# A three-layer GCN with an attention layer: layers as adj @ (h @ W), operands supplied transposed, bias and ReLU in one activation

## Chip, cores, metric

One core of a Trainium2 chip. The metric is the device time of one execution in microseconds (us), the median of several runs. Spans and durations come from the profile of one execution; a span is some 1.8 us shorter than the time of the same execution.

## The reference, cut

64 graphs of 256 nodes, 512 features, all float32.

```python
# layer 0: three GCN layers, then residual and layer norm
h = relu(adj @ (x @ W1) + b1)
h = relu(adj @ (h @ W2) + b2)
x = layernorm(x + adj @ (h @ W3) + b3)
# layer 1: graph attention with one weight per node
q, k = split(x @ Wqk);  v = x @ Wv
agg = adj @ (k * mask)
w = mask / sqrt(512) * rowsum(q * agg)
x = layernorm(x + softmax_over_nodes(w) * v)
```

Both kernels form M = Wq Wk^T once on the chip, so that w = mask/sqrt(512) * rowsum((x M) * (adj @ (mask x))).

## The kernel before

TensorE multiplies a stationary `lhsT` (transposed) by a moving `rhs`. The columns counted below are those of `rhs`. Two graphs (a pair) are handled together, and layer 1 of a pair ends inside the next pair's turn.

```python
    def transpose_adj(i, aj, k):
        pt = psum.tile([P, NH, N], FP, name="pa", tag="mm")
        for m in range(NH):
            for h in range(NH):
                nc.tensor.transpose(pt[:, m, h * P:(h + 1) * P], aj[:, k, h, m * P:(m + 1) * P], ident)
        aT = work.tile([P, NH, N], FP, name="aT", bufs=4)
        nc.scalar.copy(aT, pt)
        # ... aTm = aT times the mask, on GpSimd

    def aggregate(h_in, aT):                  # (adj @ h).T, features on partitions
        # ... for f, m:
                    nc.tensor.matmul(pz[:, j, :], lhsT=h_in[:, m, f * P:(f + 1) * P], rhs=aT[:, m, :], ...)
        # ... pz copied to zT, half by VectorE and half by ScalarE

    def project(srcT, w, h):                  # 128 rows of src @ w
        for f in range(DC):
            nc.tensor.matmul(pp, lhsT=srcT[:, f, h * P:(h + 1) * P], rhs=w[:, f, :], ...)

    def hidden(zT, n):
        # ... pp = project(zT, wl[n], h)
            nc.vector.tensor_tensor(t, pp, bl[n], op=OP.add)
            nc.scalar.activation(hn[:, h, :], t, AF.Relu)

    for i in range(NP + 1):
        # ... loads of pair i + 1
            aTs = [transpose_adj(i, aj, k) for k in ks]
        if last is not None:
            sm = softmax_rows(last[2])        # transposes the scores (pw), softmax
        if i < NP:
            zs = [aggregate(xt[:, k], aTs[k][0]) for k in ks]
        # ...
        if last is not None:
            s = softmax_cols(sm)              # transposes back (ps)
            for k in ks:
                layer1_out(i - 1, k, last[0][k], last[1][k], s)   # x1 @ Wv, sum, norm, store
        # ... two hidden layers, layer 3, layer norm, scores of pair i
```

## Time and profile before

| | before |
|---|---|
| time, us (first three runs; 3231.38 with the fourth) | 3231.34 (3231.33 to 3231.42) |
| span of the profiled run, us | 3230.6 |
| TensorE busy | 100% |
| VectorE, ScalarE, GpSimd busy | 32%, 17%, 9% |
| one pair of graphs in the steady state, us | 99.85 |

The page's first part gives busy time by engine (PE is TensorE, PEld its weight loads, DVE VectorE, ACT ScalarE, POOL GpSimd); the slices show whether that holds throughout; the chain says what the end of the program waited for. The prediction shows the lines. In the chain in order of time a row is start, length and what ran: with a TensorE that never rests, the chain accounts for the whole time of the program.

### The profile page before, as it was taken

How to read it: one execution, taken by the hardware profiler on the slowest of the kernel's cores; microseconds unless marked ns; L12 is line 12 of the kernel's file. 1: busy time of each engine (PE TensorE's matmuls, PEld its weight loads, DVE VectorE, ACT ScalarE, POOL GpSimd, SP SyncE). 2: the span in 40 equal slices, each digit the busy share in tenths (PEclk: the TensorE clock that was granted, in tenths of full speed). 3: DMA queues.
4: the chain of work that ended last, by engine and by line, in shares of the span. 5: the costliest groups of instructions: out<-in, count | busy, mean ns of one | idle time of the engine just before them, and what ended most of it. 6: DMA issues, size and time to landing. Idle time of an engine off the chain costs nothing.

```text
span 3230.6 us, 23926 instructions
## 1 busy us (share of the span) xinstructions
PE 3215.3 (100%) x9666; PEld 1753.3 (54%) x9666; DVE 1033.9 (32%) x2055; ACT 561.7 (17%) x970; POOL 276.0 (9%) x262
## 2 busy tenths in 40 slices
PE   8999999999999999999999999999999999999999
PEld 5555555555555555555555555555555555555554
DVE  1332323323333233233332332323323333333233
ACT  2111111111111111111111111111111111111111
POOL 1110011110111101111001110011110111101110
PEclk9999999999999999999999999999999999999999
DMA  3110001000000000010000000001000001000000
GB/s 134 33 33 20 26 20 33 33 20 26 20 33 33 20 26 21 32 33 26 26 27 20 33 30 23 26 20 33 33 20 26 20 33 33 20 26 20 26 14 13
DMA packets 54509, 92.55 MB, mean 29 GB/s; under 512 B 2240, under 2 KB 18688, under 8 KB 54400
## 3 DMA queue, kind: packets, MB, share of 16 engines
q1 hardware_dynamic: 54400, 91.04, 8.3%
q8 instruction: 76, 1.25, 0.2%
q14 instruction: 33, 0.27, 0.0%
HBM read 57.48 MB, written 33.55 MB: 28 GB/s over the span
## 4 chain that ended last, share of the span: by engine, by line
PE 100%; DMA 0%; DVE 0%; SPq 0%; DVEq 0%; issue 0%; ACT 0%
PE pp L150 68%; PE pz L138 21%; PE pg L208 7%; PE px L193 2%; PE pa L121 1%; PE pt L113 0%; PE pw L224 0%; PE ps L239 0%; DMA mask_n<-in_nodemask 0%; PE pt L103 0%; DVE r L248 0%; DVE st L167 0%; DVE o L174 0%; SPq L49 0%; DVEq L304 0%
## 5 line engine op out<-in xcount | busy, mean ns | idle before, releaser
L150 PE MATMUL pp<-w,zT 128*128 128x512 f32 x3072 | 1334.0, 592 | 0.0
L150 PEld LDWEIGHTS pp<-w,zT 128*128 128x128 f32 x3072 | 583.7, 190 | 707.4 <-issue 704.1
L138 PE MATMUL pz<-aT,hn 128*128 128x256 f32 x2048 | 452.5, 379 | 0.0
L150 PE MATMUL pp<-m_qk,x1T 128*128 128x512 f32 x1024 | 449.9, 592 | 0.0
L150 PE MATMUL pp<-wv,x1T 128*128 128x512 f32 x1024 | 448.3, 595 | 0.0
L138 PEld LDWEIGHTS pz<-aT,hn 128*128 128x128 f32 x2048 | 389.1, 190 | 80.2 <-issue 30.6
L159 DVE TENSOR_TENSOR t<-pp,b 128x512 f32<-128x512 f32 x256 | 177.1, 692 | 626.5 <-PE pp L150 626.5
L127 POOL TENSOR_SCALAR aTm<-aT,mask_t 128x256 f32<-128x256 f32 x128 | 117.0, 932 | 2817.8 <-ACT aT L123 2817.8
L150 PEld LDWEIGHTS pp<-m_qk,x1T 128*128 128x128 f32 x1024 | 194.6, 190 | 244.9 <-issue 244.9
L150 PEld LDWEIGHTS pp<-wv,x1T 128*128 128x128 f32 x1024 | 191.8, 190 | 229.5 <-issue 229.0
L160 ACT ACTIVATE hn<-t 128x512 f32<-128x512 f32 x256 | 161.3, 630 | 782.0 <-DVE t L159 782.0
L141 DVE COPY zT<-pz 128x512 f32<-128x512 f32 x192 | 132.9, 692 | 470.2 <-PE pz L138 470.2
L216 DVE SCALAR_TENSOR_TENSOR prod<-pp,mask_s,g 128x512 f32<-128x512 f32 x128 | 96.1, 751 | 499.2 <-PE pp L150 499.2
L138 PE MATMUL pz<-aT,xt 128*128 128x256 f32 x1024 | 231.3, 384 | 0.0
L208 PE MATMUL pg<-x,aTm 128*128 128x512 f32 x512 | 230.3, 592 | 0.0
L138 PEld LDWEIGHTS pz<-aT,xt 128*128 128x128 f32 x1024 | 193.2, 191 | 31.0 <-ACT aT L123 5.6
L170 ACT ACTIVATE sd<-mv,eps 128x2 f32<-128x2 f32 x128 | 37.9, 296 | 836.8 <-DVE mv L168 836.8
L167 DVE BATCH_NORM_STATS2 st<-r 128x6 f32<-128x512 f32 x256 | 177.5, 693 | 7.7
L248 DVE SCALAR_TENSOR_TENSOR r<-pp,s,x 128x512 f32<-128x512 f32 x128 | 96.1, 751 | 219.4 <-PE pp L150 219.4
L143 ACT COPY zT<-pz 128x512 f32<-128x512 f32 x192 | 111.6, 581 | 296.2 <-PE pz L138 296.2
L269 POOL TENSOR_TENSOR xt<-xt,b 128x512 f32<-128x512 f32 x128 | 159.3, 1264 | 25.1 <-PE pz L138 20.4
L181 DVE TENSOR_TENSOR r<-pp,xt 128x512 f32<-128x512 f32 x128 | 88.5, 692 | 227.5 <-PE pp L150 218.9
(45 smaller groups left out, 893.2 us busy)
## 6 DMA issues: line engine op xcount, KB each, us to landing
xt<-in_x SPq DMA_DIRECT2D x32, 1024.0 KB, 5.4
out<-o SPq DMA_DIRECT2D x64, 512.0 KB, 2.8
aj<-in_adj SPq DMA_DIRECT2D x32, 512.0 KB, 3.8
w<-in_L_gnn_W SPq DMA_DIRECT2D x3, 1024.0 KB, 10.6
wqk<-in_L_gnn_Wqk SPq DMA_DIRECT2D x4, 512.0 KB, 11.9
wv<-in_L_gnn_Wv SPq DMA_DIRECT2D x1, 1024.0 KB, 12.3
b<-in_L_gnn_b SPq DMA_DIRECT2D x3, 256.0 KB, 11.1
mask_n<-in_nodemask SPq DMA_DIRECT2D x1, 64.0 KB, 6.2
```

The source lines that it names most:

```text
L127: nc.gpsimd.tensor_scalar(aTm[:, m, :], aT[:, m, :], mask_t[:, m, b:b + 1], None, op0=OP.mult)
L138: nc.tensor.matmul(pz[:, j, :], lhsT=h_in[:, m, f * P:(f + 1) * P], rhs=aT[:, m, :], start=(m == 0), stop=(m == NH - 1))
L141: nc.vector.tensor_copy(zT[:, 2 * fp:2 * fp + 2, :], pz)
L143: nc.scalar.copy(zT[:, 2 * fp:2 * fp + 2, :], pz)
L150: nc.tensor.matmul(pp, lhsT=srcT[:, f, h * P:(h + 1) * P], rhs=w[:, f, :], start=(f == 0), stop=(f == DC - 1))
L159: nc.vector.tensor_tensor(t, pp, bl[n], op=OP.add)
L160: nc.scalar.activation(hn[:, h, :], t, AF.Relu)
L167: nc.vector.bn_stats(st[:, h, :], src[:, h, :])
L208: nc.tensor.matmul(pg, lhsT=aTm[:, m, h * P:(h + 1) * P], rhs=x1[:, m, :], start=(m == 0), stop=(m == NH - 1))
L216: nc.vector.scalar_tensor_tensor(prod, py, mask_s[:, h, b:b + 1], gs[h], op0=OP.mult, op1=OP.mult, accum_out=w[:, h, k:k + 1])
L248: nc.vector.scalar_tensor_tensor(r[:, h, :], pv, s[:, h, k:k + 1], x1[:, h, :], op0=OP.mult, op1=OP.add)
L269: nc.gpsimd.tensor_tensor(xt[:, k, h, :], xt[:, k, h, :], bl[2], op=OP.add)
```

## The change

Its intent: take the adjacency transposes off TensorE, make bias and ReLU one ScalarE instruction that reads PSUM, and use wide matmuls in layer 3. To that end the features go through W first, and x and the adjacency are laid out transposed by the host. Cut to its core:

```diff
+    def product(srcT, w, name):
+        dst = work.tile([P, NH, PAIR, D], FP, name=name, tag="prod", bufs=3)
+        # ... for g, m: pp = four matmuls over f, lhsT=srcT[:, f, g, m-th 128], rhs=w[:, f, :]
+                if m:
+                    nc.vector.tensor_copy(dst[:, m, g, :], pp)
+                else:
+                    nc.scalar.copy(dst[:, m, g, :], pp)
+    def aggregate_relu(s, aT, bc):
+        # ... for f, g, m:
+                    nc.tensor.matmul(pz[:, g, :], lhsT=s[:, m, g, f * P:(f + 1) * P], rhs=aT[:, g, m, :], ...)
+            nc.scalar.activation(hT[:, f], pz, AF.Relu, bias=bc[:, f:f + 1])
+    def aggregate_residual(s, aT, xb):
+        # ... for g, n, m:
+                    nc.tensor.matmul(pr, lhsT=aT[:, g, m, n * P:(n + 1) * P], rhs=s[:, m, g, :], ...)
+                nc.vector.tensor_tensor(xb[:, g, n, :], pr, xb[:, g, n, :], op=OP.add)
-    # transpose_adj, aggregate, project, hidden (shown above)
     for i in range(NP + 1):
+        # with x, aT, rows of x loaded for pair i; "last" is pair i - 1
+            s1 = product(xt, w1, "s1")
+            x1T = transpose_x1(x1)                    # last
+            hT = aggregate_relu(s1, aT, b1c)
+            y = product(x1T, m_qk, "y")               # last
+            scores(i - 1, x1, y, aTm, w)              # last
+            v = product(x1T, wv, "v")                 # last
+            sm = softmax(w)                           # last
+            s2 = product(hT, w2, "s2")
+            s = softmax_cols(sm)                      # last
+            layer1_out(i - 1, x1, v, s)               # last
+        hT = aggregate_relu(s2, aT, b2c)
+        s3 = product(hT, w3, "s3")
+        aggregate_residual(s3, aT, xn)
+        layernorm(x1, xn)
```

## The prediction

> **What bounds the kernel now.** I read the page's busy table and slices first, then the chain that ended last, then the groups, then that chain in order of time for one pair of graphs and for the end. The page says that TensorE never rests:
>
> ```profile
> PE 3215.3 (100%) x9666; PEld 1753.3 (54%) x9666; DVE 1033.9 (32%) x2055; ACT 561.7 (17%) x970; POOL 276.0 (9%) x262
> PE   8999999999999999999999999999999999999999
> PEclk9999999999999999999999999999999999999999
> PE 100%; DMA 0%; DVE 0%; SPq 0%; DVEq 0%; issue 0%; ACT 0%
> ```
>
> Line one is busy us, share and instructions of each engine; the fourth is the chain by engine. VectorE, ScalarE, GpSimd and the DMA are a third busy or less and absent from the chain. Only three things can move the time: fewer columns through TensorE, a new gap on it, and the two ends. The groups (busy, mean ns) of the parts concerned:
>
> ```profile
> L150 PE MATMUL pp<-w,zT 128*128 128x512 f32 x3072 | 1334.0, 592 | 0.0
> L138 PE MATMUL pz<-aT,hn 128*128 128x256 f32 x2048 | 452.5, 379 | 0.0
> L121 PE MATMUL pa<-ident,aj 128*128 128x128 f32 x256 | 34.1, 277 | 0.0
> ```
>
> The last column but one is the trap. 3072 times 592 ns is 1819 us, but the group was busy 1334 us: consecutive matmuls overlap, so the mean of one is not what it costs. The chain in order of time (start, length, what) gives the step; here from one pair of the steady state:
>
> ```profile
> 113.77 0.87 PE pa L121 x8
> 114.64 0.30 PE pw L224 x2
> 114.95 7.11 PE pz L138 x32
> 122.06 0.21 PE ps L239 x2
> 122.27 27.66 PE pp L150 x64
> 149.93 6.91 PE pz L138 x32
> 156.84 13.73 PE pp L150 x32
> 191.21 0.87 PE px L193 x8
> 192.08 3.44 PE pg L208 x8
> ```
>
> A 512-column record steps by 13.73/32 = 0.429 us, a 256-column one by 6.91/32 = 0.216 us (half), a 128-column transpose by 0.109 us. Cost is columns, nothing per instruction. (A matmul of the program leaves two records, a transpose one.) One pair lasts 222.12 - 122.27 = 99.85 us, from the same chain; 32 pairs are 3195 us of the 3231.
>
> **What the Trainium skill says.** "FP8 and Floating Point Precision", section "TensorE Precision Notes", says that true FP32 takes four passes through the array. The trace agrees: two records of 0.429 us for 512 columns are 1.68 ns per column; four passes at the 2.4 GHz that "TensorE: Matmul & The Clock Gate" gives for a busy array would be 1.67. The same page, section "What happens when you issue a matmul", says that the next weights are loaded while a matmul streams. The trace agrees down to 256 columns: a weight load lasts 190 ns, the 256-column step is 216 ns. Its section "The HAM clock gate" says that the array runs at half clock until some 3.4 us of work have passed, and again after idleness of that length. The first transposes and first aggregate agree: 1.90 us against 0.87 and 8.72 us against 6.91. The granted clock row doesn't show it. "Perfetto Trace Analysis", section "Matmuls", says that larger matmuls are more efficient; between 256 and 512 columns of this kernel the trace doesn't show that.
>
> **The change part by part**, per pair, by the chain's steps.
>
> Association. Before, each of three layers is 32 records of 256 columns (aggregate) and 32 of 512 (project). Afterwards each is the same 32 of 512 first; layers one and two then aggregate with 32 of 256, features on partitions again. Swapping the order saves no arithmetic, because the width is 512 in and out. Layer three aggregates with 16 records of 512: 16 x 0.429 = 6.86 us in place of 6.91. Saved: 0.05 us.
>
> Adjacency transposes: 8 transposes, 0.87 us, gone and on the path. Saved: 0.87 us. With them goes one ScalarE copy per graph (589 ns), off the path.
>
> Softmax. The scores' row transpose (pw) now follows the product with Wv, so it no longer waits for the last score: 0.30 us becomes about 0.21. Saved: 0.09 us. The 0.2 us that TensorE loses after each of these tiny transposes (7.11 against 6.91, 27.66 against 27.46) I leave in.
>
> Bias and ReLU. 256 VectorE additions (692 ns, 177 us) and 256 ScalarE activations (630 ns, 161 us) become 256 ScalarE activations straight from PSUM, but all five products are now copied out, half by each engine. None of it is on the path: ScalarE idles 782 us ahead of its old ReLU and VectorE 627 us ahead of its addition, waiting for others.
>
> Loads. 0.5 + 1 MB in per pair become 2.5 MB; with 1 MB out that is 3.5 MB in 99 us, some 37 GB/s, against 384 GB/s moved in the busiest stretch at the start. Hidden. Single buffers: the row copy of x is reloaded only after the layer norm of the pair before, but is needed most of a period later; a 1 MB load lands in 5.4 us.
>
> Sum in the middle: 0.87 + 0.05 + 0.09 = 1.01 us, times 32 = 32 us less.
>
> Start. Before, TensorE begins at 8.1 us, when the mask lands. Now it needs W1 and x transposed, 2.1 MB, where 1.6 MB lay ahead of the mask; 0.5 MB at 385 GB/s is 1.3 us. Then the mask must land before the first aggregate; with 6 MB ahead of it that is near 20 us, and the first product ends near 25. Cost: 1.3 us, the half-clock start being paid in both.
>
> End. Here is the chain after the last matmuls of before:
>
> ```profile
> 3213.79 9.65 PE pp L150 x22
> 3223.44 0.03 issue
> 3223.47 0.76 DVE r L248
> ...
> 3225.73 0.55 DVE o L174
> 3226.28 0.46 DVEq L304
> ```
>
> From TensorE's end to the end of the span are 7.2 us: the softmax is hidden under the product with Wv, and only one graph's half and its layer norm stick out. The change serialises this. First, there is no new pair to fill in for the layer norm of layer 0: last addition 0.69, statistics 0.69 + 0.18, square root 0.30, reciprocal 0.17, four scalings of 0.54 and hand-overs: 4.3 us of idle TensorE, then perhaps half clock for one window, 1.7 us. Second, softmax follows everything: maximum 0.41, exponential 0.47 + 0.18, reciprocal 0.15, scaling 0.39, hand-overs: 1.8 us; column transposes drained and copied 0.4; then for four half-graphs 3.0 of weighted sums, 3.5 of statistics, 0.5 root and reciprocal, 2.1 scaling: about 11.5 us in all. Third, one store of 1 MB rather than two of 0.5: 3.9 us plus 0.5 MB at 385 GB/s is 5.3. So 16.8 in place of 7.2. Cost of the end: 9.6 + 4.3 + 1.7 = 15.6 us.
>
> Total: 3231.3 - 32.3 + 1.3 + 15.6 = 3215.9 us. About half of the middle's gain is given back at the ends. I say 3215.
>
> **The rivals.**
>
> Wider matmuls pay. By the means of 592 and 379 ns, layer three would save 32 x 379 - 16 x 592 = 2.7 us per pair, 85 us in all; with the transposes that makes about 3110 us, faster by over 3%. Against it stands the overlap shown above: the steps are 0.429 and 0.216. I give it two in a hundred.
>
> A new wait on ScalarE. In the instruction order of the changed kernel, the square root of the layer-1 norm stands between the third and fourth ReLU of the second aggregate, and the third layer's product needs all four. Counting from the end of the second product: VectorE copies 0.7, takes the softmax columns 0.2, four weighted sums 3.0, statistics 3.5 and the root comes at about 7.9 us. The fourth aggregate is done at 0.2 + 6.9 = 7.1, its ReLU then ends at 8.5; TensorE needs it three matmuls (six records, 2.6 us) after 7.1, at 9.7. So 1.2 us of slack. If VectorE ran 2 us longer there, TensorE would lose some 0.8 us per pair, 25 us: 3240, still within 2%. That this must cost over 3 us per pair to be slower by 2% makes it unlikely.
>
> The small stalls go. If the 0.2 us after the row and column transposes came from the transposed adjacency or the old order, up to 0.4 us per pair would go too: 13 us, 3202.
>
> A late load. The order of the queue puts the store of one pair between loads of the next. For a load to hold TensorE up it would have to land over 60 us late; the profile shows 5.4 us for 1 MB. If it happened each pair the time would exceed 3300.
>
> **Range and chances.** Work that cannot go away is 192 records of 0.429, 64 of 0.216 and 16 transposes, with pw and ps 98.4 us per pair; with the preparation of Wq Wk^T (3.49 + 13.74 us) and no gaps but the start, that is over 3170, so faster by 2% (under 3168) is all but excluded. The range runs from all small stalls gone and a cheaper end (3198) to half a microsecond more of new stalls per pair with the end as worked out (3226). Faster 0.02, same 0.965, slower 0.015.
>
> **What would show each step.** Right: TensorE again near 100%, the period near 98.8 us; adjacency transposes absent; the new 512-column aggregates step 0.43 us and the whole third aggregate lasts 6.9 us; weights loaded behind matmuls as before; VectorE idle ahead of its copies, waiting for TensorE; a gap near 4 us ahead of the last pair's transposes of x1, and 16 to 17 us from the last product to the end. Wrong: TensorE waiting each pair for the fourth ReLU or for a load; a period under 98.2 or over 99.5 us; an end as short as before; the third aggregate clearly under 6.8 us.

## The result

3205.81 us (3205.10 to 3205.96, 4 runs) against 3231.38: ratio 0.992, 95% interval 0.9906 to 0.9934, within 2%. A ratio is the mean time of one kernel's fast runs over that of the other's of the same rounds, so not quite the ratio of the medians quoted. The time lies inside the range and 9 us under the 3215 predicted.

Busy table, slices and chain by engine of the changed kernel, as shown of before:

```profile
PE 3177.7 (99%) x8898; PEld 1629.2 (51%) x8898; DVE 903.7 (28%) x1863; ACT 523.7 (16%) x842; POOL 274.8 (9%) x262
PE   8999999999999999999999999999999999999997
PE 99%; DVE 0%; DMA 0%; issue 0%; ACT 0%; DVEq 0%; SPq 0%
```

TensorE still sets the time; only its last slice has fallen, from 9 to 7. Its chain through a pair in the steady state:

```profile
246.18 0.22 PE pw L165 x2
246.40 13.74 PE pp L89 x32
260.13 0.21 PE ps L180 x2
260.34 7.10 PE pz L104 x32
...
281.18 6.87 PE pr L115 x16
...
303.53 6.91 PE pz L104 x32
```

The adjacency transposes (pa) are gone. The row transpose of the scores takes 0.22 us instead of 0.30, and what follows it loses nothing (13.74); what follows the column transpose (ps) still loses 0.2 us (7.10 against 6.91). The wide aggregate of layer 3 (pr) takes 6.87 us for 16 records, the narrow ones 6.91 for 32. From 161.75 to 3119.48 us lie 30 pairs: 98.59 us each, against 99.85, measured likewise from 122.27 to 3117.66. That is 1.26 us less, 37.7 us in 30 pairs. The span fell by 26.5 only, so the two ends gave 11 us back. The end of the changed kernel in the same chain: the gap ahead of the last pair's transposes of x1, the first product after it and the last one:

```profile
3149.51 0.56 DVE x L132
3150.07 0.04 issue
3150.11 3.05 PE px L141 x16
3153.19 14.52 PE pp L89 x32
...
3174.58 13.75 PE pp L89 x32
```

TensorE stood 2.9 us for the layer norm (the waits say PE px waited for DVE x once, 2.9 us), then the transposes took 3.05 us instead of 1.75 and the product 14.52 instead of 13.73: 5.0 us in all. The slow stretch is a lower granted clock: here are three stretches of the changed kernel, 3150.10 to 3150.86 us, 3150.86 to 3154.27 and 3154.27 to 3157.00, as the profile sums them up: length, busy time of each engine in the order of the page, and, third from the right, the granted clock.

```profile
3150.10:3150.86 0.76, 0.75 (x7) 0.71 (x8) 0.76 (x2) 0.00 (x0) 0.00 (x0) 1.00 0.03 11
3150.86:3154.27 3.41, 3.38 (x14) 2.46 (x13) 1.85 (x4) 1.07 (x2) 0.00 (x0) 0.50 0.00 0
3154.27:3157.00 2.73, 2.73 (x8) 1.30 (x7) 0.00 (x0) 0.00 (x0) 0.00 (x0) 1.00 0.00 0
```

From the end of the last product, 3188.3 us, to the end of the span are 15.8 us, against 7.2 before: 8.6 more.

### The profile page after: what moved, and what is told of

It is laid out like the page before. It is cut to its first block, busy times and chain, and to the rows that moved or that the text cites. A ratio compares the mean times of both kernels' runs of the same rounds, so it can differ in the third digit from the quotient of the medians.

```text
span 3204.1 us, 21715 instructions
## 1 busy us (share of the span) xinstructions
PE 3177.7 (99%) x8898; PEld 1629.2 (51%) x8898; DVE 903.7 (28%) x1863; ACT 523.7 (16%) x842; POOL 274.8 (9%) x262
## 4 chain that ended last, share of the span: by engine, by line
PE 99%; DVE 0%; DMA 0%; issue 0%; ACT 0%; DVEq 0%; SPq 0%
PE pp L89 69%; PE pz L104 14%; PE pg L155 7%; PE pr L115 7%; PE px L141 2%; PE pt L223 0%; DMA xt<-in_xT 0%; PE ps L180 0%; PE pw L165 0%; DVE st L124 0%; PE pt L213 0%; DVE xn L117 0%; DVE x L188 0%; DVE x L132 0%; DVE mv L125 0%
## 5 line engine op out<-in xcount | busy, mean ns | idle before, releaser
L89 PE MATMUL pp<-w,hT 128*128 128x512 f32 x2048 | 889.4, 592 | 0.0
L89 PEld LDWEIGHTS pp<-w,hT 128*128 128x128 f32 x2048 | 386.7, 190 | 462.1 <-issue 459.7
L104 PE MATMUL pz<-aT,s 128*128 128x256 f32 x2048 | 455.9, 381 | 0.0
L89 PE MATMUL pp<-w,xt 128*128 128x512 f32 x1024 | 447.7, 595 | 8.1 <-DMA xt<-in_xT 8.1
L92 DVE COPY s<-pp 128x512 f32<-128x512 f32 x192 | 132.8, 692 | 1006.4 <-PE pp L89 1006.4
L104 PEld LDWEIGHTS pz<-aT,s 128*128 128x128 f32 x2048 | 384.1, 190 | 50.6 <-issue 0.5
L89 PEld LDWEIGHTS pp<-w,xt 128*128 128x128 f32 x1024 | 195.6, 191 | 254.4 <-issue 254.4
L267 POOL TENSOR_TENSOR xn<-xn,b3r 128x512 f32<-128x512 f32 x128 | 158.0, 1265 | 1920.0 <-DMA xn<-in_xN 1902.5
L94 ACT COPY s<-pp 128x512 f32<-128x512 f32 x192 | 112.5, 586 | 798.9 <-PE pp L89 798.9
L115 PE MATMUL pr<-s,aT 128*128 128x512 f32 x512 | 224.9, 592 | 0.0
```

What stands on the lines that cost most here:

```text
L89: nc.tensor.matmul(pp, lhsT=srcT[:, f, g, m * P:(m + 1) * P], rhs=w[:, f, :], start=(f == 0), stop=(f == DC - 1))
L92: nc.vector.tensor_copy(dst[:, m, g, :], pp)
L94: nc.scalar.copy(dst[:, m, g, :], pp)
L104: nc.tensor.matmul(pz[:, g, :], lhsT=s[:, m, g, f * P:(f + 1) * P], rhs=aT[:, g, m, :], start=(m == 0), stop=(m == NH - 1))
L115: nc.tensor.matmul(pr, lhsT=aT[:, g, m, n * P:(n + 1) * P], rhs=s[:, m, g, :], start=(m == 0), stop=(m == NH - 1))
L267: nc.gpsimd.tensor_tensor(xn[:, g, h, :], xn[:, g, h, :], b3r, op=OP.add)
```

## The experiments

Theory: TensorE pays for every column in turn. The transposes are the gain, the rest of the change is neutral in the middle, and its end costs 13 us. Rivals: the gain comes from association, wide matmuls or the fused activation; the transposes were hidden; the end is set by the store.

### The transposes alone

The kernel before, with the adjacency laid out by the host.

```diff
-                nc.tensor.transpose(pt[:, m, h * P:(h + 1) * P], aj[:, k, h, m * P:(m + 1) * P], ident)
-        aT = work.tile([P, NH, N], FP, name="aT", bufs=4)
-        nc.scalar.copy(aT, pt)
+        aT = aj[:, k]
```

> The kernel before with one part of the change alone: the adjacency comes transposed from the host, its 8 transposes and 2 copies per pair are gone; association, biases, order and end stay. Theory (TensorE pays every column in turn): 0.87 us per pair less, 28 us in all, 3203 us; up to 0.3 us per pair more (3194) if the small stalls around the scores' row transpose go with it, since the scheduler now puts two aggregates between its two halves. Rival 1 (the transposes were hidden or their place is taken by a wait for the last score): 3225 to 3231. Rival 2 (most of the change's gain is the new association): again near 3231.

3196.55 us, ratio 0.9891 (0.9876 to 0.9906): 35 us less with this alone. The chain between the products with M and with Wv in this kernel:

```profile
211.47 0.11 PE pw L219
211.58 0.87 PE pz L133 x4
212.45 0.20 PE pw L219
212.65 6.04 PE pz L133 x28
```

The compiler's scheduler put the first two matmuls of the aggregate (four records) between the halves of the row transpose, so the second half no longer stands waiting for the last score. A pair takes 98.73 us (112.74 to 211.47), 1.12 less; the transposes are 0.87 of it. The rivals that call the transposes hidden, or the gain the association's, fall.

### The row transpose further from the last score

```diff
-            sm = softmax_rows(last[2])
-            zs = [aggregate(xt[:, k], aTs[k][0]) for k in ks]
+            zs = [aggregate(xt[:, 0], aTs[0][0])]
+            sm = softmax_rows(last[2])
+            zs.append(aggregate(xt[:, 1], aTs[1][0]))
```

> As the first run, and the scores' row transpose moved between the two graphs' aggregates, where the last score is long there. Theory (the 0.3 us per pair beyond the transposes that the change won is the wait for the last score and the drained pipe after it): the row transpose no longer waits, 3193 to 3197 us, and the aggregates of a pair take 6.9 us plus at most 0.2. Rival (the small loss follows each tiny transpose wherever it stands): the same time as the first run within 3 us.

3193.06 us, ratio 0.9881 (0.9864 to 0.9897), another 3.5 us.

```profile
210.55 3.45 PE pz L133 x16
214.00 0.22 PE pw L219 x2
214.22 3.46 PE pz L133 x16
217.68 0.21 PE ps L234 x2
217.89 27.66 PE pp L145 x64
```

The two halves of the aggregate add up to 6.91 us: the loss around the row transpose is gone where nothing is awaited, while the 0.2 us after the column transpose stays (27.66). A pair takes 98.64 us, within 0.05 of the changed kernel. So the 0.2 us after the row transpose, which the prediction left in, went with the wait for the last score; the rival, a loss after each tiny transpose, is right for ps alone.

### Everything but the transposes

The changed kernel, with the adjacency loaded as it is.

```diff
             s1 = product(xt, w1, "s1")
+            aT = transpose_adj(aj)      # eight transposes, two ScalarE copies
```

> The changed kernel with one part undone: the adjacency comes as it is and is transposed on TensorE between the first product and the transposes of x1. Association, fused bias and ReLU, order and end as changed. Theory: 8 steps of 0.109 us per pair come back, 28 us, 3234 us, so that new association, fused activation and new end together are worth nothing or slightly less than nothing. Rival (association or fused activation carries the gain): 3206 to 3215 us.

3233.67 us, ratio 1.0005 (0.999 to 1.002). It runs 27.9 us above the changed kernel, which is 32 times 0.87, and like the kernel before. In its chain:

```profile
204.98 0.87 PE pa L233 x8
205.85 1.75 PE px L141 x16
```

New association, fused activation, new order and new end together changed nothing that can be told from zero: what the order won in the middle the end took.

### Narrower matmuls

The changed kernel with all products cut into pieces of CW columns, 256 and then 128 instead of 512.

```diff
-                    nc.tensor.matmul(pp, lhsT=srcT[:, f, g, m * P:(m + 1) * P], rhs=w[:, f, :],
+                for c in range(0, D, CW):
+                    for f in range(DC):
+                        nc.tensor.matmul(pp[:, c:c + CW], lhsT=srcT[:, f, g, m * P:(m + 1) * P], rhs=w[:, f, c:c + CW],
```

> The changed kernel with all five products (320 records of 512 columns for two pairs) in 256-column matmuls, so twice as many instructions and weight loads for the same columns. Theory (cost is columns, weights load behind): 320 records of 0.216 in place of 160 of 0.429 us per pair, 0.5 us more, some 16 us in all, 3222 us. Rival (the duration of one record is what it costs, 381 against 592 ns): 27 us per pair more, over 4000 us.

> The same in 128-column matmuls, four times as many. Theory with its limit (a weight load lasts 190 ns and cannot lie behind a stream of 107 ns): 640 records of 0.19 us in place of 160 of 0.429 per pair, 53 us more, some 4900 us. If columns alone counted even here: 0.107 us a record, under 3240 us.

256 columns: 3217.83 us, 12 above the changed kernel. 128 columns: 3294.81 us, 89 above it. One product in the chain, first at 256, then at 128:

```profile
332.18 13.81 PE pp L91 x64
```

```profile
338.77 14.29 PE pp L91 x128
```

Twice as many instructions cost 0.08 us per product, four times as many 0.56. The rival that a record costs its mean duration (it would have made over 4000 us) is dead. My own limit for 128 columns was wrong too, by 1600 us, and through the very trap that the prediction warns of for matmuls. The groups of that kernel, busy and mean ns:

```profile
L91 PE MATMUL pp<-w,hT 128*128 128x128 f32 x8192 | 925.3, 275 | 0.0
L91 PEld LDWEIGHTS pp<-w,hT 128*128 128x128 f32 x8192 | 922.5, 192 | 3.0 <-issue 0.5
```

A weight load has a duration of 192 ns, but 8192 of them fill 922.5 us, 113 ns each: loads overlap with each other as matmuls do. The Trainium skill's "TensorE: Matmul & The Clock Gate", section "LDWEIGHTS (loading the stationary operand)", gives a load in ns as its columns over 1.2; for 128 columns that is an estimate of 107 ns, nearer to this step than to the duration. So even at 128 columns the loads lie nearly behind the matmuls: a record steps by 0.112 us, where its share of the wide product would be 0.107.

### Bias and ReLU apart

```diff
-            nc.scalar.activation(hT[:, f], pz, AF.Relu, bias=bc[:, f:f + 1])
+            nc.vector.tensor_scalar(t, pz, bc[:, f:f + 1], None, op0=OP.add)
+            nc.scalar.activation(hT[:, f], t, AF.Relu)
```

> The changed kernel with the fused activation undone: VectorE adds the bias from PSUM into a tile of its own, ScalarE takes the ReLU. VectorE has 70% of its time free. Rival (idle engines take it for nothing, as the prediction said of bias and ReLU): 3206 us within 3. Theory: in the instruction order the additions for the second aggregate stand in VectorE's queue behind the weighted sums, the statistics and, for the fourth, the scalings of the layer-1 norm, so the fourth ReLU ends near 12.2 us after the second product where TensorE needs it at 9.7: 2.5 us per pair, 78 us in all, 3284 us, and TensorE is seen to wait in the third product.

3222.00 us, ratio to before 0.9969 (0.9954 to 0.9983), 16 us above the changed kernel: neither nothing nor 78. Its chain, and then the fourth ReLU in the timeline of ScalarE:

```profile
366.45 0.63 ACT hT L108
...
367.13 14.00 PE pp L89 x32
```

```profile
371.55 0.63 ACT L108 ACTIVATE hT<-t 128x512 f32<-128x512 f32 x1 [1.82 <-DVE t L107]
```

The fourth ReLU came as late as worked out, 12.6 us after the second product ended (359.56), behind VectorE's layer norm. But TensorE lost only 0.53 us per pair: 0.27 waiting for the first ReLU, 0.27 in the product (14.00 against 13.73), all of it at the product's first two records. The scheduler had interleaved three accumulation groups here, so that six matmuls (5.2 us) precede the first that needs the fourth ReLU; in the changed kernel it is three, as predicted. The weights of the seventh were loaded at 372.23 us, just after the ReLU ended at 372.18, and the matmul lost nothing. I had read the orders of VectorE and ScalarE and not TensorE's. What the late ReLU costs with the old matmul order was not run. What is shown: undoing the fused activation, new matmul order included, costs 16 us, because the first addition stands behind the weighted sums and statistics of layer 1 in VectorE's queue.

### The last pair, graph by graph

The changed kernel; the last pair alone goes as in the kernel before.

```diff
+        if i == NP - 1:
+            finish(i, hT, aT, xn)   # per graph: W3 product, aggregate, norm; then per graph: x1T, y, scores;
+            break                   # v of half 0, softmax, v of half 1, columns, v of graph 1; four stores
```

> The changed kernel with only its last pair arranged graph by graph, as in the kernel before: one graph's layer norm lies beside the other's products, the softmax lies beside the product with Wv, the result is stored in four pieces. Theory (the change gave back 5.0 us of TensorE standing or at half clock ahead of the last transposes of x1 and 8.6 us after its last product): 13.6 us less than the changed kernel, 3192 us, with 7 us from the last product to the end. Rival (the end is bound by the store and the fixed ending of the program, so order matters little): 3202 to 3206 us.

3193.02 us, ratio 0.988 (0.9865 to 0.9895): 12.8 us under the changed kernel. That the store sets the end, falls. First the chain, then TensorE's timeline of the same stretch:

```profile
3147.99 0.59 ACT x1T L290
...
3178.17 3.64 PE pv L305 x8
...
3185.67 0.67 DVE x L316
```

```profile
3178.10 7.13 PE L305 MATMUL pv<-wv,x1T 128*128 128x512 f32 x16
```

The chain leaves TensorE at 3181.8 us for VectorE's queue, but TensorE has eight more records to go: by their step its last product ends near 3185.1, and the span at 3191.8. That is the 7 us that were forecast (6.7), 9 less than in the changed kernel. With the 5.0 us of the gap it would make 14; the order by graph loses some of that again on TensorE, about 1 us of it ahead of the two products with M, each of which is held up some 0.5 us by ScalarE's copy of x1T (3147.99).

### The start as well

```diff
-    w1 = load_w(W1, "w1");  loaded = load_pair(0)
+    # W1 on one queue and the first x on another, in four pieces each
+    # first product preceded by WARM = 8 matmuls of the identity
-        # 32 transposes of Wq, Wk
+        # Wq, Wk laid out transposed by the host
```

> The kernel with the last pair by graph, and the start shortened as well: W1 and the first x come in four pieces each over two queues, TensorE multiplies the identity eight times while they travel, and Wq and Wk come transposed from the host, so their 32 transposes go. Theory (3 us of start before the first product, 3.1 us at half clock, 3.5 us of transposes): 6 to 9 us under the kernel with the last pair by graph, about 3184 us, 1.5% under the kernel before. Rival (the first product is held by the bytes of its loads, whatever their pieces, and the clock follows the first real products): only the 3.5 us of transposes, 3188 us or more.

3190.50 us (0.9872, 0.9855 to 0.9888), a miss: 2.5 us under the run before, less than the 3.5 us of the transposes. The profiled execution, the fastest of the four (3189.02), shows that the start won little:

```profile
2.12 10.17 DMA xt<-in_xT
12.33 11.43 PE pp L101 x26
```

The product began at 6.2 us, but the last piece of x landed at 12.3 us, where the whole load had landed at 8.0. So the first product ended at 23.76 us, only 1.3 earlier than in the changed kernel. Why the other three executions took 1.2 to 1.9 us longer, no trace shows. So once more with whole loads and 22 matmuls of the identity:

> As the kernel with both ends, but W1 and the first x are loaded whole over one queue again, and TensorE multiplies the identity 22 times while they travel. Theory: in pieces the last piece of x landed at 12.3 us, whole it lands at 8.0, so the pieces cost what their early start won; whole, and with the array at full clock from the first product, the first product takes 13.7 us from 8.1 instead of 16.9 and the mask's transpose starts near 21.9 instead of 23.8 (pieces) or 25.0 (changed kernel): 2 us under the kernel with both ends, 3188.5 us. Rival (multiplying the identity does not bring the clock up, or the mask or W2 is then awaited): the first product again takes over 16 us or a new wait follows, 3191 us or more.

```profile
1.34 7.42 PE pp L92 x44
8.76 13.74 PE pp L94 x32
22.50 0.27 PE pm L205 x2
```

3187.54 us, ratio 0.9863 (0.9846 to 0.9879), the fastest version, 44 us under the kernel before and 18 under the changed one. The first product takes 13.74 us, where it took 16.89 in the changed kernel: after 7.4 us of identity matmuls the product steps at full rate from its first record on. They run 0.6 us too long (8.76 against 8.14).

## Why the prediction was right

The mechanism held: TensorE stayed the bound, columns set its time, the transposes were the gain, and about a third of it went back at the end. The sum, 3215.9, was 10 us too high, through mis-sized terms.

- **Transposes, 0.87 us per pair**: right. Put back alone they cost 27.9 us, 0.87 a pair.
- **Association, 0.05 us per pair**: right; 6.87 against 6.91 us, and with everything else but the transposes it is worth nothing. The rival of wide matmuls fell as argued, and the runs with narrow ones show it.
- **Softmax, 0.09 us per pair**: mis-sized. The term measured some 0.3, because the 0.2 us that TensorE lost after the row transpose was part of the wait for the last score, not of the tiny transpose. This third rival (13 us) happened in part: with 1.26 us per pair instead of 1.01, 8 us of the 10 are here.
- **Bias and ReLU off the path**: right for the change, but not for the reason given. The idle time of ScalarE and VectorE proves nothing: VectorE was busy 28% of the time, and putting the addition on it cost 16 us.
- **The square root between the ReLUs**: no wait came. The fourth ReLU ended 8.5 us after the second product, the number worked out, by two errors that cancelled: VectorE was faster, as its instructions overlap too when they run back to back (four weighted sums of 747 ns took 2.74 us, not 3.0), and ScalarE first loaded a table for the root, 1.28 us, which I had left out. The need at 9.7 us was read rightly: three matmuls precede in the compiled order.
- **Start, 1.3 us**: measured about 0.3. The first product began at 8.14 us, the same as the mask's transpose before (8.12), with 0.5 MB more ahead of it; the half-rate start cost 3.2 us against 2.8.
- **End, 15.6 us**: measured 13.6. The gap was 2.9 us and not 4.3, as each transpose waits only for its own block of x1; with what followed it, 5.0 against 6.0. The half clock came as foreseen, for one window of 3.4 us. From the last product to the end, 15.8 against 16.8. Undoing this end alone won 12.8.

These terms come to 11 us, and the sum was 10 too high. The remaining microsecond lies between spans and times: the profiled execution of the kernel before was about 1 us longer than its median (a span of 3230.6 and 1.8 make 3232.4), so the spans fell by 26.5 us and the medians by 25.6.

The rival of wide matmuls was added up wrongly: 3231 less 85 and 28 is 3118, not 3110, and the cost of the end is missing from it. Nothing else rests on it.

## What to carry to other kernels

Where one engine is busy throughout, count what it pays for by the step from one instruction to the next in the chain, never by the mean duration, be it of matmuls, of weight loads or of vector instructions back to back: with that, a rewrite that looks large may be seen to move only one term. Then look at the ends: an order that fills every gap in the middle with the next item's work has none to fill them with for the last item, and here giving that item its own order won half as much as the whole change. Idle time of an engine is no proof that work put there is free; what counts is where it comes in that engine's queue, and whether the bound engine has other work to take meanwhile.

## What the Trainium skill lacked or had wrong

- "Perfetto Trace Analysis", section "Identifying the Most-Contended Engine", says to use the busy share of LDWEIGHTS, beside MFU (the share of peak arithmetic reached), in place of that of matmuls. With products in 128 columns that share rose from 51% to 90% and the time by 2.8%: the loads' durations overlap (192 ns each, 113 ns apart), so their busy share overstates what they cost just as that of matmuls does.
- "TensorE: Matmul & The Clock Gate", section "The HAM clock gate", asks for an idle window of about 3.4 us before the clock halves, and calls the window free-running. Here TensorE stood for 2.9 us (3147.2 to 3150.1), and the next seven transposes still stepped by 0.109 us; from 3150.86 on they stepped by 0.213, with a granted clock of 0.50 for 3.41 us. So a gap shorter than the window was enough in this run; whether the seven transposes counted as work is not shown. At the start of the changed kernel the product stepped by 0.853 us instead of 0.429 from 8.14 to about 14.0 us, longer than the 3.4 us of work that the prediction took from the page; the views show a granted clock of 1.00 there.
- No page gives the step of float32 matmuls by width. The runs show, per record (each matmul leaves two), 0.429 us for 512 columns, 0.216 for 256 and 0.112 for 128.
- No page says what a transpose of two columns costs its successor: 0.2 us on TensorE after each ps, in the chains of before, after and both runs without transposes.
